# Two tiles' worth of lead for the projections of tile 5, and a second projection step per unit for tiles 4 to 7, in a graph-and-attention kernel

## The chip, the cores and the metric

The kernel runs on one core of one Trainium2 chip. The metric is the time of one execution on the device in microseconds. Instructions run on five engines that each work through their own queue in order: TensorE (PE, matmuls), VectorE (DVE), ScalarE (ACT), GpSimd (POOL) and SyncE (SP, which issues the DMAs). They wait for each other through semaphores.

## The reference, cut to what matters

Two layers run over 3327 nodes with 256 features. Each layer has a graph step over a dense 3327 x 3327 adjacency matrix and a feed-forward step: a mixture of experts in the first layer, and in the second a causal attention with four heads of width 64, each with four query "experts", followed by a small feed-forward part. The change touches only this last step:

```
sx = einsum('bsh,ndh->bnsd', x, hl_w) + hl_b
q = einsum('bnsd,neod->bneso', sx, wq)
k = einsum('bnsd,nod->bnso', sx, wk)
v = einsum('bnsd,nod->bnso', sx, wv)
scores = einsum('bnesd,bntd->bnest', q, k) * d ** 0.5 + causal
att = softmax(scores, axis=-1)
qkv = einsum('bnest,bntd->bnesd', att, v)
qkv = where(sx == 0, 0.0, qkv)
...
mixed = einsum('bnsed,bnse->bnsd', out.reshape(b, nh, s, ne, d), gs)
hn = layernorm(mixed + resid, ln_g, ln_b)
...
```

Here x is the normalised input, b is 1, n counts the heads, e the four query experts, s the query rows and t the key rows. All is computed in 32-bit floats.

## The kernel before, in words

The rows are cut into 26 tiles of 128 (NT). The second layer's last step is the function heads() at line 854, which takes from about 985 us to the end. Its engines are wrapped so that every engine keeps the order in which the program issues its instructions; the order written in the Python code is therefore the order in each queue.

*Units, chunks, rounds.* A unit is one tile t and one head h (line 1387). A unit's keys are cut into t // 4 + 1 chunks of up to 512 (span, line 1012), so tiles 0 to 3 have one chunk a unit, tiles 4 to 7 two, tiles 8 to 11 three. The main loop (line 1438) handles one chunk k per pass; this text calls a pass a round, and names chunks as tile.head.chunk, such as 4.1.0. A round does, in this order:

- drain_to(wanted(k)): VectorE copies scores from PSUM to SBUF with their maxima (drain, line 1034) until it is k + 3 + t // 4 chunks on; drains that find nothing filled call fill_next() first.
- attend(k) on TensorE: probabilities times values, into the PSUM tile po.
- turn(k + 1) on VectorE: the transpose of the next chunk's probabilities.
- values(k + 2): four DMAs on SP into vr (three buffers); weigh(k + 2): the exponentials on ScalarE, two ahead of the rest of the round and two behind it if the chunk is not a unit's first, else all four behind.
- back() of the unit that ended in the round before: TensorE turns its output (ptO), ScalarE copies it to qkv and glp.
- over(), if this chunk is the unit's last: po times a mask to ot, for tiles below 5 on VectorE, later by ScalarE and POOL.
- run(preps) and run(tails), if no unit ended in the round before or the tile is below 8: one step of each projection under way, and one step of each tail (norms and feed-forward of finished tiles).
- the rest of weigh(k + 2), and fill_next() (line 1407): TensorE multiplies queries and keys of the next chunk into four tiles pqk of PSUM (fill, line 1019).

*PSUM.* po takes four banks. The pool with the tag "b" has four buffers of a bank; pqk, all projections, transposes, ptO and the tails share it. One fill takes all four.

*Projections.* prepare() (line 907) is a generator with nine steps for a tile:

1. load x (SP)
2. statistics of its rows (three VectorE instructions)
3. power, subtract and multiply to xn (POOL)
4. transpose xn, evict to xt
5. psxt = hl_w times xt; sxt and the mask nz (four ScalarE instructions)
6. four DMAs sxd <- nz; pv, evict to v
7. pk, two evictions to kt; four DMAs vs <- v
8. pq, two evictions to qt (scaled by 8)
9. transpose of sxt, evict to sx

Only after step 9 does the tile's entry in ready hold qt. empty() (line 877) picks ScalarE or VectorE for an eviction by two running sums of estimated load. For tiles below AHEAD, qt is placed in a buffer of the pool "sc" (nine buffers, which otherwise hold the scores) and is called qts in the profile; for the others it has a tag of its own with two buffers.

*When a projection is begun.* begin(u) (line 1389) is called by fill_next() for a unit's first chunk. For head 0 of tile t it first calls run(preps) until the tile's qt is ready, and then begins other tiles: the next tile (t + 1) if that is AHEAD or more, and tile t + 2 if that is below AHEAD (tile 0 begins 1 and 2). With AHEAD = 5, tiles up to 4 are begun two tiles ahead, and tiles from 5 on are begun one tile ahead. As fills run four to five chunks ahead of attend in tiles 4 to 7, begin(5) falls into the round of chunk 4.2.0, begin(6) into that of 5.2.0, and so on; begin(4) falls into the round of 3.1.0.

Of the kernel before, what the change touches and what calls it, by code (L numbers as in the profile page):

```python
# [101 lines left out]
class Net:  # L102
# [751 lines left out]
    def heads(self, xs, vs, out):  # L854
# [3 lines left out]
        with ExitStack() as ctx:  # L858
# [48 lines left out]
            def prepare(t, res):  # L907
# [65 lines left out]
                yield  # L973
                if t < AHEAD:

# [20 lines left out]
            def run(gens):  # L996

                gens[:] = [g for g in gens if next(g, None) is None and g.gi_frame is not None]

            tails, preps, ready = [], [], {}  # L1000
            AHEAD = 5

            def later(n, gen):

# [14 lines left out]
            def fill(u, g):  # L1019

                t, h = u["t"], u["h"]
                lo, n = span(t, g)
                n *= P
                pq = u["pq"] = []
                for i in range(2):
                    pq += [ps.tile([P, BLK], F32, tag="b", name="pqk") for _ in range(2)]
                    for k in range(2):
                        r = ds(64 * k, 64)
                        nc.tensor.matmul(
                            pq[2 * i + k][:, :n], u["qt"][r, h, i, :], kt[r, h, ds(lo * P, n)],  # L1030
                            start=True, stop=True,
                        )
# [27 lines left out]
            def weigh(u, g, experts):  # L1060

                n = span(u["t"], g)[1] * P
                q = ready[u["t"]]
                if u["h"] == g == 0 and 0 in experts:
                    q["den"] = sm.tile([P, 16, 7], F32, tag="den", name="aden", bufs=2)
                for k in experts:
                    e = u["sc"][g][:, k, :n]
                    nc.scalar.activation(
                        e, e, AF.Exp, bias=u["nmax"][:, k : k + 1],
                        accum_out=q["den"][:, 4 * u["h"] + k, g : g + 1],  # L1070
                    )
                    load["act"] += 0.26 + 0.00088 * n

            def values(u, g):

                lo, n = (4 * i for i in span(u["t"], g))
                v = u["v", g] = vrp.tile([P, 16, 64], F32, tag="vr", name="vr")
                for q in range(4):
                    nc.sync.dma_start(out=v[ds(Q * q, Q), :n, :], in_=vs[u["h"], :, lo : lo + n, :])

            def turn(u, g):


                n = span(u["t"], g)[1] * P
                w = u["sc"][g][:, :, :n]
                nc.vector.transpose(w, w)
                load["dve"] += 0.1 + 0.00417 * n
# [7 lines left out]
            def attend(u, g):  # L1095


                t = u["t"]
                w, v = u["sc"][g], u["v", g]
                lo, n = (4 * i for i in span(t, g))  # L1100
                for b2 in range(0, n, 2):
                    for k in range(2):
                        for q in range(4):
                            r, b = ds(Q * q, Q), b2 + k

                            after = 4 * t + q - lo
                            if b > after and t:
                                continue
                            nc.tensor.matmul(
                                po[ds(64 * k, 64), q, :, :], v[r, b, :], w[r, :, ts(b, Q)],  # L1110
                                start=(g == b2 == 0), stop=(b + 2 > after if t else b2 == 2),
                            )

            def over(u):

                u["ot"] = tl.tile([P, 4, P], F32, tag="ot", name="ot", bufs=1)
                to = u["ot"].rearrange("p e (q i) -> p q e i", q=4)
                there = u["sxd"][:, u["h"] : u["h"] + 1, :]
                if u["t"] < 5 or u is units[-1]:

                    nc.vector.tensor_tensor(
                        to, po,
                        there.rearrange("p o (q i) -> p q o i", q=4).to_broadcast([P, 4, 4, Q]),
                        ALU.mult,
                    )
                    load["dve"] += 0.7
                else:
                    nc.scalar.copy(to, po)
                    nc.gpsimd.tensor_tensor(
                        u["ot"], u["ot"], there.to_broadcast([P, 4, P]), ALU.mult  # L1130
                    )
                    load["act"] += 0.6

            def back(u):


                h = u["h"]
                r = ready[u["t"]]
                if h == 0:
                    r["qkv"] = tl.tile([P, 4, 4, 64], F32, tag="qkv", name="qkv", bufs=2)  # L1140
                    r["glp"] = sm.tile([P, 4, 4, 4], F32, tag="glp", name="glp", bufs=3)
                pt = ps.tile([P, 4, 68], F32, tag="b", name="ptO")
                for e in range(4):
                    nc.tensor.matmul(
                        pt[:, e, :], u["ot"][:, e, :], igw[:, h, e, :], start=True, stop=True
                    )
                nc.scalar.copy(r["qkv"][:, h, :, :], pt[:, :, :64])
                nc.scalar.copy(r["glp"][:, h, :, :], pt[:, :, 64:])
                load["act"] += 0.55
                if u["t"] == NT - 1:  # L1150
                    if h % 2:
                        tails.append(last_tail(u["t"], h // 2, u["sx"], r))
                elif h == 3:
                    while len(tails) > 4:
                        run(tails)
                    tails.append(tail(u["t"], u["sx"], r["qkv"], r["glp"], r["den"]))
# [232 lines left out]
            def begin(u):  # L1389

                t = u["t"]
                if u["h"] == 0:
                    if t == 0:
                        for _ in prepare(0, ready.setdefault(0, {})):
                            pass
                    while preps and "qt" not in ready[t]:
                        run(preps)
                    begun = [t + 1] if AHEAD <= t + 1 < NT else []
                    if t + 2 < AHEAD:
                        begun = [t + 2] if t else [1, 2]  # L1400
                    for i, n in enumerate(begun):
                        preps.append(later(4 * i, prepare(n, ready.setdefault(n, {}))))
                u.update(ready[t])
# [3 lines left out]
            def fill_next():  # L1407
                nonlocal filled
                if filled < len(chunks):
                    u, g = chunks[filled]  # L1410
                    if g == 0:
                        begin(u)
                    fill(u, g)
                    filled += 1

            def drain_to(n):
                nonlocal drained
                while drained < min(n, len(chunks)):
                    if filled == drained:
                        fill_next()  # L1420
                    drain(*chunks[drained])
                    drained += 1

            def wanted(k):

                return k + 3 + chunks[min(k + 2, len(chunks) - 1)][0]["t"] // 4
# [11 lines left out]
            for k, (u, g) in enumerate(chunks):  # L1438
                ahead = chunks[k + 2] if k + 2 < len(chunks) else None
                drain_to(wanted(k))  # L1440
                attend(u, g)
                if k + 1 < len(chunks):
                    turn(*chunks[k + 1])
                if ahead:
                    values(*ahead)
                    if ahead[1]:
                        weigh(*ahead, range(2))
                if ended:
                    back(ended)
                last = u if g == u["t"] // 4 else None  # L1450
                if last:
                    over(u)
                if not ended or u["t"] < 8:
                    run(preps)
                    run(tails)
                ended = last
                if ahead:
                    weigh(*ahead, range(2 if ahead[1] else 0, 4))
                if filled == drained:
                    fill_next()  # L1460
            back(ended)
            while tails:
                run(tails)
# [2 lines left out]
class Experts:  # L1466
# [340 lines left out]
    def run(self, beside):  # L1807
        net, tc, S = self.net, self.tc, self.SLOTS
        nc = self.nc
        with ExitStack() as ctx:  # L1810
# [80 lines left out]

            AHEAD = 5
            for i in range(AHEAD):
                take(i)
# [4 lines left out]
            for i in range(S + 2):  # L1899
                if i + AHEAD == self.SURE:  # L1900
                    while rest:
# [115 lines left out]
```

## Time and profile before

| What | Value |
|---|---|
| Time, median of 3 runs (lowest to highest) | 2946.86 us (2946.50 to 2949.19) |
| Profiled execution | 2943.34 us |
| Its span, first to last instruction | 2941.60 us |
| Mean granted TensorE clock | 0.977 |
| Heads stage | about 985 us to the end |
| pq (step 8) of tiles 4, 5, 6, 7, 8 starts at | 1076.51, 1123.33, 1171.93, 1215.91, 1264.40 us |
| Evictions qts <- pq, qt <- pq | 10 (8 ScalarE, 2 VectorE), 42 (ScalarE) |

The page of a profile gives busy times of each engine, the chain of work that ended last, and the costliest groups of instructions. Besides it the trace can be asked for stretches of time (busy microseconds of each engine in each, with the granted clock), for the instructions of an engine in order of time with the wait ahead of each and what released it, and for sums of waits. In an order of time a line reads: start, duration (or that of the merged group), engine, line, operation, output <- inputs with shapes, count, and in brackets the idle time of the engine just before it with what ended it. Ends of matmuls are modelled. All work of the heads stage is recorded under line 61, that of the wrapper, so instructions are told apart by their tile names.

### The profile page before, as it was taken

How to read it: one execution, taken by the hardware profiler on the slowest of the kernel's cores; microseconds unless marked ns; L12 is line 12 of the kernel's file. 1: busy time of each engine (PE TensorE's matmuls, PEld its weight loads, DVE VectorE, ACT ScalarE, POOL GpSimd, SP SyncE). 2: the span in 40 equal slices, each digit the busy share in tenths (PEclk: the TensorE clock that was granted, in tenths of full speed). 3: DMA queues.
4: the chain of work that ended last, by engine and by line, in shares of the span. 5: the costliest groups of instructions: out<-in, count | busy, mean ns of one | idle time of the engine just before them, and what ended most of it. 6: DMA issues, size and time to landing. Idle time of an engine off the chain costs nothing. (4 is left out here: it accounts for less than half of the span.)

```text
span 2941.6 us, 125324 instructions
## 1 busy us (share of the span) xinstructions
PE 2652.3 (90%) x53422; PEld 1963.2 (67%) x53422; DVE 2398.5 (82%) x5619; ACT 1811.3 (62%) x5128; POOL 973.1 (33%) x1448
## 2 busy tenths in 40 slices
PE   7999988878989898999999999999989999999995
PEld 5878877757767676666666666666666666666664
DVE  5102643589999587889989999999999999999997
ACT  6420135555554477778777777777767677676674
POOL 5441634622141146544334323322122222122121
PEclk9999999999999799999999999999999999999998
DMA  9994568647775232333333433333433433433432
GB/s 372 357 322 148 176 209 279 209 171 264 268 250 177 73 92 75 115 97 116 115 103 109 123 112 110 113 114 110 123 113 109 117 115 115 117 115 108 116 110 78
DMA packets 258188, 449.70 MB, mean 153 GB/s; under 512 B 58816, under 2 KB 156608, under 8 KB 257504
## 3 DMA queue, kind: packets, MB, share of 16 engines
q1 hardware_dynamic: 245536, 417.50, 45.7%
q0 software_dynamic: 6576, 18.02, 1.6%
q8 instruction: 421, 6.90, 1.0%
q10 hardware_dynamic: 5520, 6.18, 0.7%
q14 instruction: 135, 1.11, 0.1%
HBM read 393.37 MB, written 25.88 MB: 143 GB/s over the span
## 5 line engine op out<-in xcount | busy, mean ns | idle before, releaser
L61 ACT ACTIVATE sc<-sc,anmax 128x512 f32<-128x512 f32 (+3 forms) x1568 | 1039.9, 668 | 109.0 <-DVE anmax L61 108.9
L61 PEld LDWEIGHTS po<-sc,vr 32*64 32x64 f32 x43728 | 661.1, 131 | 390.9 <-DVE sc L61 233.8
L61 PE MATMUL po<-sc,vr 32*64 32x128 f32 x43728 | 764.0, 275 | 113.6 <-DVE sc L61 74.8
L61 DVE STREAM_TRANSPOSE sc<-sc 128x2048 f32<-128x2048 f32 (+3 forms) x392 | 816.4, 2083 | 26.2 <-ACT sc L61 25.3
L61 PE MATMUL pqk<-kt,qt 64*128 64x512 f32 (+1 forms) x2944 | 738.4, 582 | 18.6 <-ACT qt L61 5.3
L61 DVE TENSOR_SCALAR_CACHE_REDUCE sc<-pqk 128x512 f32<-128x512 f32 (+2 forms) x1152 | 654.9, 623 | 51.2 <-PE pqk L61 49.7
L61 PEld LDWEIGHTS pqk<-kt,qt 64*128 64x128 f32 x2944 | 299.3, 185 | 230.3 <-issue 99.2
L61 PE MATMUL acc<-wh,p 128*128 128x259 f32 x1352 | 309.1, 386 | 35.6 <-DVE p L61 35.5
L61 PEld LDWEIGHTS acc<-wh,p 128*128 128x128 f32 x1352 | 253.3, 190 | 93.4 <-DVE p L61 53.4
L61 PE MATMUL acc<-y,pan 128*128 128x256 f32 x1352 | 304.3, 385 | 11.4 <-DMA pan<-in_adjt_dram 9.7
L61 ACT ACTIVATION_READ_ACCUMULATOR sc<-sc,anmax 128x1 f32 x1568 | 299.0, 191 | 0.0
L61 POOL TENSOR_TENSOR ot<-ot,sxd 128x512 f32<-128x512 f32 x83 | 105.7, 1273 | 582.2 <-ACT ot L61 568.8
L61 PEld LDWEIGHTS acc<-y,pan 128*128 128x128 f32 x1352 | 258.4, 193 | 52.4 <-issue 16.7
L61 DVE CUSTOM_DVE_ANT_0 sc<-pqk,mask 128x512 f32<-128x512 f32 (+3 forms) x416 | 242.3, 636 | 24.2 <-PE pqk L61 23.7
L61 ACT ACTIVATE u<-u,d 128x512 f32<-128x512 f32 (+1 forms) x182 | 125.2, 688 | 159.2 <-DVE u L61 159.0
L61 DVE SCALAR_TENSOR_TENSOR u<-bc,d 128x512 f32<-128x512 f32 (+1 forms) x182 | 136.1, 748 | 0.1
L61 DVE SCALAR_TENSOR_TENSOR p<-pan,u 128x512 f32<-128x512 f32 (+1 forms) x182 | 127.5, 701 | 10.3 <-PE acc L61 6.1
L61 ACT ACTIVATE junk<-ar 128x1664 bf16<-128x1664 f32 x52 | 82.7, 1591 | 65.2 <-DMA ar<-in_adj_dram 64.2
L61 ACT COPY qkv<-ptO 128x256 f32<-128x256 f32 x104 | 38.4, 369 | 136.2 <-PE ptO L61 136.0
L61 PE MATMUL ptO<-igw,ot 128*128 128x68 f32 x832 | 117.4, 284 | 4.5 <-issue 2.7
L61 PEld LDWEIGHTS ptO<-igw,ot 128*128 128x128 f32 x832 | 102.5, 193 | 23.3 <-issue 17.4
L61 DVE CUSTOM_DVE_ANT_0 sg<-sg,dst 128x1664 bf16<-128x1664 bf16 (+2 forms) x56 | 99.6, 1787 | 1.2 <-ACT dst L61 1.0
(340 smaller groups left out, 3024.8 us busy)
## 6 DMA issues: line engine op xcount, KB each, us to landing
vr<-vs SPq DMA_DIRECT2D x976, 128.0 KB
ar<-in_adj_dram SPq DMA_DIRECT2D x104, 832.0 KB
vr<-vs SPq DMA_DIRECT2D x544, 96.0 KB
pan<-in_adjt_dram SPq DMA_DIRECT2D x156, 256.0 KB
pan<-in_adjt_dram SPq DMA_DIRECT2D x26, 1024.0 KB
pan<-in_adjt_dram SPq DMA_DIRECT2D x20, 832.0 KB
w1e<-w SPq DMA_DIRECT2D x59, 256.0 KB
took<-places SPq DMA_DIRECT2D x59, 129.0 KB
```

The source lines that it names most:

```text
L61: made = make(*args, **kw)
```

## The change

AHEAD becomes 6. Tile 5 is thereby begun in begin(3), in the round of chunk 2.1.0, instead of in begin(4), and its qt is placed in the pool "sc". begin(4) begins nothing. At the end of each round that is a unit's last, in tiles 4 to 7, run(preps) is called once more, behind fill_next().

```
@@ -998,7 +998,7 @@
                 gens[:] = [g for g in gens if next(g, None) is None and g.gi_frame is not None]
 
             tails, preps, ready = [], [], {}
-            AHEAD = 5
+            AHEAD = 6
 
             def later(n, gen):
 
@@ -1458,6 +1458,9 @@
                     weigh(*ahead, range(2 if ahead[1] else 0, 4))
                 if filled == drained:
                     fill_next()
+                if last and 4 <= u["t"] < 8:
+
+                    run(preps)
             back(ended)
             while tails:
                 run(tails)
```

With these steps the order of the projections becomes, as it can be read off the loop (steps in brackets are those of the added call):

| Round | before | changed |
|---|---|---|
| 2.2.0 to 3.0.0 | tile 4: 6, 7, 8 | tile 4: 6, 7, 8; tile 5: 1, 2, 3 |
| 3.1.0 | tile 4: 9 | tile 4: 9; tile 5: 4 |
| 3.2.0, 3.3.0, 4.0.0 | tile 5: 1, 2, 3 | tile 5: 5, 6, 7 |
| 4.0.1 | tile 5: 4 | tile 5: 8 [9] |
| 4.1.0, 4.1.1 | tile 5: 5, 6 | none |
| 4.2.0 | tile 5: 7, then 8 and 9 in begin(5) | none |
| 4.2.1 | tile 6: 1 | tile 6: 1 [2] |
| 4.3.0, 4.3.1 | tile 6: 2, 3 | tile 6: 3, 4 [5] |
| 5.0.0, 5.0.1 | tile 6: 4, 5 | tile 6: 6, 7 [8] |
| 5.1.0, 5.1.1 | tile 6: 6, 7 | tile 6: 9, none |
| 5.2.0 | tile 6: 8, then 9 in begin(6) | none |

Tiles 7 and 8 follow the pattern of tile 6. Tile 9, before its first steps in the rounds of tile 7, gets two of the added calls (its steps 2 and 5); from tile 8 on the added call is not made.

More of the change, by code (lines that the diff above doesn't have):

```diff
@@ L1000, in heads @@
             tails, preps, ready = [], [], {}
-            AHEAD = 5
+            AHEAD = 6
             def later(n, gen):
@@ L1460, in heads @@
                     fill_next()
+                if last and 4 <= u["t"] < 8:
+                    run(preps)
             back(ended)
```

## The prediction

> **What bounds the kernel now.** I read the page's busy line first, then a table of stretches over the heads stage, then VectorE's, TensorE's and ScalarE's order of time around the tiles that the change names. All recorded work carries the helper's line 61, so I place it by tile names.
>
> Share of each engine over the span, from the page:
>
> ```profile
> PE 2652.3 (90%) x53422; PEld 1963.2 (67%) x53422; DVE 2398.5 (82%) x5619; ACT 1811.3 (62%) x5128; POOL 973.1 (33%) x1448
> ```
>
> No engine is full on average, so the stage decides. Stretches (start:end, length, then busy us of PE, weight loads, DVE, ACT, POOL with counts, granted clock, DMA share, GB/s):
>
> ```profile
> 1060.00:1100.00 40.00, 37.62 (x853) 27.79 (x852) 36.05 (x98) 29.38 (x98) 19.98 (x29) 1.00 0.28 78
> 1100.00:1140.00 40.00, 34.16 (x589) 24.83 (x588) 26.90 (x78) 30.59 (x115) 23.21 (x36) 0.91 0.29 81
> 1140.00:1180.00 40.00, 37.63 (x768) 26.55 (x768) 32.08 (x89) 30.84 (x107) 27.50 (x40) 0.96 0.28 80
> 1180.00:1220.00 40.00, 37.70 (x849) 26.36 (x848) 34.17 (x89) 30.92 (x102) 24.74 (x36) 1.00 0.38 107
> 2000.00:2400.00 400.00, 367.85 (x10904) 248.99 (x10890) 388.05 (x852) 283.36 (x861) 96.87 (x135) 1.00 0.39 114
> ```
>
> Late in the stage VectorE is the bound (388 of 400). In the stretch of tiles 4 to 8, PE (94%) and DVE (80 to 90%) are both near full and hand work to each other every round. One stretch falls out: 1100 to 1140, where DVE does 26.9 us, PE loses 3.5, and the clock was 0.91. VectorE's longest waits, in order of time (start, us, what, [wait <- releaser]):
>
> ```profile
> 1116.03 1.25 DVE L61 STREAM_TRANSPOSE sc<-sc 128x1024 f32<-128x1024 f32 x1 [2.96 <-ACT sc L61]
> 1121.57 0.38 DVE L61 TENSOR_REDUCE l1ns<-fx 128x4 f32<-128x256 f32 x1
> 1128.74 0.56 DVE L61 TENSOR_SCALAR_CACHE_REDUCE sc<-pqk 128x384 f32<-128x384 f32 x1 [6.79 <-PE pqk L61]
> ...
> 1174.72 0.56 DVE L61 TENSOR_SCALAR_CACHE_REDUCE sc<-pqk 128x384 f32<-128x384 f32 x1 [2.85 <-PE pqk L61]
> ...
> 1218.91 0.69 DVE L61 TENSOR_SCALAR_CACHE_REDUCE sc<-pqk 128x512 f32<-128x512 f32 x1 [1.33 <-PE pqk L61]
> ...
> 1267.19 0.56 DVE L61 TENSOR_SCALAR_CACHE_REDUCE sc<-pqk 128x384 f32<-128x384 f32 x1 [1.11 <-PE pqk L61]
> ```
>
> The last four are the first drain of tiles 5, 6, 7 and 8. TensorE before the one at 1128:
>
> ```profile
> 1117.51 1.18 PE L61 MATMUL pqk<-kt,qts 64*128 64x384 f32 x4 [1.91 <-ACT v L61]
> ...
> 1122.32 0.71 PE L61 MATMUL pk<-sxt,wk 64*128 64x128 f32 x8
> 1122.96 0.44 PE L61 MATMUL pt<-ident,fx 128*128 128x128 f32 x2
> 1123.33 1.31 PE L61 MATMUL pq<-sxt,wq 64*128 64x128 f32 x16
> 1124.57 0.44 PE L61 MATMUL pt<-ident,sxt 128*128 128x128 f32 x2
> 1127.79 1.97 PE L61 MATMUL pqk<-kt,qt 64*128 64x384 f32 x8 [2.78 <-ACT qt L61]
> ```
>
> The reader is to see steps 7 (pk), 8 (pq) and 9 (pt of sxt) of tile 5's preparation one behind the other, then PE waiting for ScalarE's eviction of qt, which stands in ScalarE's queue behind four exponentials.
>
> **What the Trainium skill says.** "TensorE: Matmul & The Clock Gate", Part 1, says that the array falls to half rate after an idle window of about 3.4 us and that the window is free-running. The trace agrees: in 8 us stretches the clock was 0.79 at 1116 to 1124, 0.81 at 1124 to 1132 and again 0.79 at 1164 to 1172, each behind a PE wait, and it was 1.00 after 1180. "PSUM — Partial Sum Buffer", Terms, gives a matmul output at most one bank of eight: po takes four, the pool "b" the other four, and one fill (4 pqk) takes all four, so any projection behind a fill waits for VectorE's first drain. "Perfetto Trace Analysis", Identifying the Most-Contended Engine, warns that PE's busy share is no measure of its headroom; so "PE near full" here is weaker evidence than the waits.
>
> **The change, part by part.** I walked the loop at line 1438 by hand; a round is one chunk. prepare() has nine steps, and each run(preps) makes one.
>
> *Tile 5 now.* Begun in begin(4), it makes steps 1 to 7 in seven rounds, and begin(5) makes 8 and 9 at once. *Changed:* begun in begin(3), it makes steps 1 to 8 in the eight rounds before 4.1.0, and 9 in the first added call. begin(5), three rounds on, finds it done. What goes:
> - The wait of 6.79. Without pk, pq and pt, PE's fill stands behind ptO and pt<-fx. DVE was free at 1121.95; PE's ptO began at 1120.51, and ptO 1.1, pt 0.4 and the first score pair 0.95 lead to about 1123.0. I leave 1.0 of the wait: 5.8 saved.
> - Of the 2.96 before the transpose at 1116: ScalarE had no gap from 1100.6 to 1118, and sxt 0.63, nz 0.84 and v 0.35 of tile 5 stood in that queue: 1.8 saved.
> - The slow clock behind it: attend's 84 matmuls took 2.84 instead of 1.64 at 1129.7, and DVE then waited 0.69 and 0.62. I take 0.7.
>
> Sum 8.3; bounds 4 (half the waits come back) to 11 (the waits, both slow windows).
>
> *What tile 5 costs earlier.* PE's six groups, 4.0 us from start to start (pt 0.3, psxt 1.05, pv 0.6, pk 0.65, pq 1.1, pt 0.3), and ScalarE's 3.8 us go to 1083 to 1106. ScalarE has 5.7 us of gaps there (1.10, 1.27, 1.26, 2.09 ahead of qkv) and takes it. PE shows gaps of 0.93, 0.51 and 0.50, so up to 2.1 is uncovered while DVE runs without a wait over 0.72. I take 1.0; bounds 0 to 2.1. The three VectorE instructions of step 2 (0.7 us) only change place. Step 3 goes to a POOL that idled 13 us before 1085. Its nine DMA issues pass earlier through SP, whose vr loads were waited for once, for 0.5 us, in 1120 to 1270: nothing. qt now lies in one of the nine "sc" buffers for ten rounds; drains run up to five chunks ahead, with tile 4's qt that makes seven: nothing. All evictions after tile 1 go to ScalarE (qt 42 of 42), and the order of load sums moves too little to alter that.
>
> *The added call for tiles 6 to 8.* Steps 2, 5 and 8 go behind the fill of a unit's last round; step 9 is made two rounds before the tile begins. Waits of 2.85, 1.33 and 1.11 (5.3 together) stand at these beginnings, but PE itself paused for only 0.31 us at each: it was busy with pq and pt (1.6 us), which remain to be done. Where PE sets the pace nothing is gained by moving them. Upper bound 5.3, and 1.7 more for half of the slow window at 1166. Against it: of the added calls eight hold matmuls (sx of 5; psxt and q of 6, 7, 8; psxt of 9). Each now stands between a fill and the next attend and needs a bank, or two for q, that DVE must first drain: 0.55 or 1.1 us, 6.0 in all (5 x 0.55 + 3 x 1.1) if DVE reaches the drain only when PE is done filling, nothing if DVE waits for the scores as at 1174. The eviction falls where ScalarE waits for ptO anyway (1.0 to 4.1 us before each qkv). I take 2.5 gained and 1.6 lost: 0.9; bounds -6 to +7.
>
> Sum: -8.3 + 1.0 - 0.9 = -8.2 us. The profiled execution took 2943.34 (span 2941.60 and 1.74 around it): 2935.1. The median shown is 2946.86, 3.5 above it; 8 off that gives 2939.
>
> **Rivals.** (1) *The wait is refilled, 0.33.* Around 1085 to 1106 PE and DVE are both near full, and tile 5's 4 us lengthen those rounds by 2.1; bank waits cost 3 to 4 beside a gain of 2 at tiles 6 to 8; half the slow windows stay (2 of the 8.3). -8.3 + 2 + 2.1 + 1.5 = -2.7: 2944. For it: the 94% of PE. Against: the clean gap at 1121 that belongs to ordering alone. Here too falls the case that the second edit does nothing, if its calls find an empty list; the walk shows that only one in four does.
> (2) *The added call blocks attend, 0.17, slower.* PE is in order, so psxt or q waiting for a bank keeps attend, back and the next fill behind it. Price: 6.0 for the drains; and if the pauses trip the slow clock once in each of the eight, eight windows of 3.4 us at half rate lose up to 1.7 us each, 13.6. -8.3 + 1.0 + 6.0 + 13.6 = +12; with half of the windows +5.5; middle +9: 2956. It decides from about 1.7 us a call: 8 x 1.7 less the 7.3 of tile 5 is 6.3, just over what counts as slower. For it: the pause of 1.91 for v at 1117 shows what one bank costs. Against: the eviction is off the fill's way here.
> (3) *All three beginnings pay too,* within the forecast: -8.3 + 1.0 - 5.3 = -12.6: 2934.
>
> **How the numbers follow.** This kernel's measurement tells 0.2%, 5.9 us, from no change. Forecast (with the third rival) 0.50: faster, 2939, its own range 2933 to 2941. First rival 0.33, within 0.2%. Second 0.17, slower; its smaller outcomes reach into the range. Range 2931 to 2952: below it lies only a gain beyond every bound but the last, above it most of the second rival.
>
> **What would show it.** Right: tile 5's first drain waits under 1.5 us instead of 6.79; qts has 12 evictions instead of 10 and qt 40 instead of 42; no slow clock between 1100 and 1135; pq of tile 5 about 1105; first drains of tiles 6 to 8 under 1 us. Wrong: new PE waits for banks directly behind a fill, with attend behind them; DVE busy below 34 of 40 in 1060 to 1100; the slow clock at new places in tiles 5 to 8.

## The result, and the profile after

The changed kernel takes 2961.21 us (median of 5, 2957.57 to 2966.76); the kernel before, timed beside it, 2946.86 (2944.14 to 2949.19). The ratio is 1.0043, 95% interval 1.0031 to 1.0056: slower by 0.43%, some 13 us. The profiled execution took 2957.57 us, span 2955.9, mean granted clock 0.972.

The busy line of the page after the change:

```profile
PE 2658.0 (90%) x53422; PEld 1969.3 (67%) x53422; DVE 2397.5 (81%) x5619; ACT 1808.9 (61%) x5128; POOL 973.1 (33%) x1448
```

Counts are those of before: nothing was added, work was moved. The loss is new idle time. The same stretches (busy us of PE, weight loads, DVE, ACT, POOL, then clock):

```profile
1060.00:1100.00 40.00, 36.94 (x794) 27.98 (x795) 34.23 (x90) 31.03 (x105) 19.55 (x29) 1.00 0.29 77
1100.00:1140.00 40.00, 34.10 (x644) 24.00 (x643) 29.74 (x88) 28.23 (x106) 23.70 (x37) 0.91 0.27 75
1140.00:1180.00 40.00, 37.60 (x771) 28.66 (x771) 28.82 (x84) 30.07 (x105) 24.65 (x36) 0.88 0.27 77
1180.00:1220.00 40.00, 34.83 (x740) 25.98 (x733) 29.72 (x79) 28.85 (x98) 19.80 (x31) 0.87 0.38 108
2000.00:2400.00 400.00, 368.45 (x10760) 249.35 (x10761) 387.02 (x847) 285.93 (x869) 98.09 (x136) 1.00 0.39 114
```

The late stage is as before. In 1100 to 1140 DVE does 2.8 us more, as it should without the wait of 6.79, but the clock is still 0.91, and from 1140 to 1220 DVE does 29 of 40 us where it did 32 and 34. Single lines of VectorE's order of time (what lies between them is left out), at the places that answer to those shown of before (the first drains of tiles 5, 6, 7 and 8 start at 1125.13, 1178.12, 1227.61 and 1276.37):

```profile
1125.13 0.54 DVE L61 TENSOR_SCALAR_CACHE_REDUCE sc<-pqk 128x384 f32<-128x384 f32 x1
1132.60 1.25 DVE L61 STREAM_TRANSPOSE sc<-sc 128x1024 f32<-128x1024 f32 x1 [5.48 <-ACT sc L61]
1178.12 0.56 DVE L61 TENSOR_SCALAR_CACHE_REDUCE sc<-pqk 128x384 f32<-128x384 f32 x1 [1.88 <-PE pqk L61]
1187.59 0.43 DVE L61 BATCH_NORM_STATS2 pst<-xres 128x6 f32<-128x256 f32 x1 [5.36 <-DMA xres<-xs]
1227.61 0.68 DVE L61 TENSOR_SCALAR_CACHE_REDUCE sc<-pqk 128x512 f32<-128x512 f32 x1
1235.74 0.43 DVE L61 BATCH_NORM_STATS2 pst<-xres 128x6 f32<-128x256 f32 x1 [3.62 <-DMA xres<-xs]
1276.37 0.55 DVE L61 TENSOR_SCALAR_CACHE_REDUCE sc<-pqk 128x384 f32<-128x384 f32 x1
1283.49 0.43 DVE L61 BATCH_NORM_STATS2 pst<-xres 128x6 f32<-128x256 f32 x1 [2.60 <-DMA xres<-xs]
```

Every wait that the change aimed at is gone or smaller. But each is followed by another one elsewhere: 5.48 for ScalarE where 6.79 went, then 5.36, 3.62 and 2.60 for a load of x, 11.6 together, where 2.85, 1.33 and 1.11 were. Counted from 0 in order, the n-th of these statistics instructions is tile n's, so the last three are tiles 7, 8 and 9. Before, none of them waited.

To see where time is lost and not only where an engine idles, I compared the start of each chunk's first drain in the two traces, and took the difference (after less before, us):

| Chunk | 3.1.0 | 4.3.0 | 5.0.0 | 5.0.1 | 6.0.0 | 6.0.1 | 7.0.0 | 7.0.1 | 8.0.0 | 8.0.1 | 8.1.2 | 9.2.0 |
|---|---|---|---|---|---|---|---|---|---|---|---|---|
| Difference | +2.0 | +5.3 | -3.6 | +1.2 | +3.4 | +9.1 | +8.7 | +12.6 | +9.2 | +12.2 | +15.9 | +15.1 |

The 2.0 at the left is there before the first changed round. Each first drain of a tile comes early against its neighbours, and the chunk after it gives the gain back and more. Below, "stage difference" is this measure from chunk 2.3.0 to chunk 9.2.0 alone (293.75 us before): +13.1 here, all of the loss. What follows chunk 9.2.0 differs between single profiles by several us, so a ratio of a few tenths of a percent and a stage difference of one profile need not agree exactly.

Besides the waits the clock is worse in this stage. Its stretch in one, before and then after:

```profile
1060.00:1300.00 240.00, 220.82 (x4957) 156.94 (x4959) 200.03 (x526) 183.35 (x618) 134.39 (x195) 0.98 0.33 93
1060.00:1300.00 240.00, 212.30 (x4567) 155.02 (x4568) 187.59 (x492) 173.16 (x588) 128.83 (x188) 0.92 0.31 88
```

By the clock's records TensorE ran at half rate for 10.2 us of this stretch before and for 37.5 after. In e1 to e16 below it was 6.8 to 37.5 us: 17.1 in e1, 30.7 in e3, 23.9 in e13, 6.8 in e15. No run takes a wait away and leaves the slow clock that goes with it, so how much of a loss is the wait and how much the clock stays open.

**The load.** POOL, SP, VectorE, TensorE and ScalarE around 1187:

```profile
1181.09 0.73 POOL L61 TENSOR_TENSOR fo<-fo,xend 128x256 f32<-128x256 f32 x1
```

```profile
1181.84 0.36 SPq L61 DMA_DIRECT2D out_dram<-fo  x1
1182.30 1.77 SPq L61 DMA_DIRECT2D vr<-vs  x4
1184.17 0.37 SPq L61 DMA_DIRECT2D xres<-xs  x1
```

```profile
1188.34 0.68 DVE L61 CUSTOM_DVE_ANT_0 sc<-pqk,mask 128x512 f32<-128x512 f32 x1
```

```profile
1189.17 1.95 PE L61 MATMUL ptO<-igw,ot 128*128 128x68 f32 x8 [4.37 <-POOL prs L61]
```

```profile
1191.16 0.37 ACT L61 COPY qkv<-ptO 128x256 f32<-128x256 f32 x1 [6.15 <-PE ptO L61]
```

The added call makes step 2 in the same round as step 1. SP issues the load at 1184.17, behind four vr and an output DMA, which waits until POOL has written fo (1181.09 and 0.73 more); x is there 3.4 us later (1187.59 less 1184.17). VectorE had been ready for it since 1182.23 (1187.59 less 5.36) and could do nothing else: the drain that empties the banks stands behind the statistics and starts at 1188.34. TensorE's ptO needs a bank, and the fill ahead of it had taken all four, so it had to wait for the first of these drains, which ends at 1189.02. The label says prs on POOL, but by the code ptO reads nothing of POOL's prs. ScalarE waits 6.15 for ptO. A single late load has stopped three engines.

**The mask.** ScalarE and POOL before VectorE's wait at 1132.60:

```profile
1129.73 0.42 ACT L61 ACTIVATE nzf<-fx 128x256 f32<-128x256 f32 x1 [5.12 <-POOL fo L61]
```

```profile
1128.98 0.73 POOL L61 TENSOR_TENSOR fo<-fo,nzf 128x256 f32<-128x256 f32 x1
```

and ScalarE's same instruction before:

```profile
1124.43 0.42 ACT L61 ACTIVATE nzf<-fx 128x256 f32<-128x256 f32 x1 [0.44 <-POOL fo L61]
```

nzf (line 1242) has one buffer. The tail of one tile writes its mask into it while POOL has yet to read the mask of the tile before. ScalarE waits 5.12 for that, with the exponentials behind it that the transpose at 1132.60 needs. Before, ScalarE waited only 0.44 for the same mask, inside the 6.79 that VectorE spent on tile 5's projection (1121.95 to 1128.74). With the change ScalarE is ready for it 0.6 us later (1124.61 against 1123.99), but POOL, at work without a pause since 1113.73, reads the old mask 5.3 us later (1128.98 against 1123.66). Why POOL came so much later was not looked into.

### The profile page after: what moved, and what is told of

It reads as the page before. It is cut to its first block, busy times and chain, and to the rows that moved or that the text cites. A ratio compares the mean times of both kernels' runs of the same rounds, so it can differ in the third digit from the quotient of the medians.

```text
span 2955.9 us, 125326 instructions
## 1 busy us (share of the span) xinstructions
PE 2658.0 (90%) x53422; PEld 1969.3 (67%) x53422; DVE 2397.5 (81%) x5619; ACT 1808.9 (61%) x5128; POOL 973.1 (33%) x1448
## 3 DMA queue, kind: packets, MB, share of 16 engines
q14 instruction: 135, 1.11, 0.1%
## 5 line engine op out<-in xcount | busy, mean ns | idle before, releaser
L61 PE MATMUL pqk<-kt,qt 64*128 64x512 f32 (+1 forms) x2880 | 722.0, 587 | 18.6 <-DVE sc L61 8.2
```

Source lines behind the costliest of these rows:

```text
L61: made = make(*args, **kw)
```

## The experiments

All ratios are to the kernel before, run on the same chip; e1 to e16 ran on three chips, on which it took 2941 to 2949 us, so where an expectation is in us it is read as a ratio to 2946.86. Stage differences are worked out from the drains' starts as above.

| Run | Edit, against after | Ratio [95%] | Stage difference |
|---|---|---|---|
| after | | 1.0043 [1.0031, 1.0056] | +13.1 |
| e1 | without the added call | 1.0008 [0.9999, 1.0017] | +1.9 |
| e2 | AHEAD 5 | 1.0034 [1.0023, 1.0045] | +8.8 |
| e3 | x loaded one round earlier | 1.0015 [1.0008, 1.0022] | +5.4 |
| e4 | no call in head 2 | 1.0057 [1.0043, 1.0071] | +19.6 |
| e5 | call in head 1 of tiles 5 to 7 only | 0.9996 [0.9987, 1.0004] | +1.1 |
| e6 | e1 with the mask later | 0.9995 [0.9988, 1.0002] | -3.8 |
| e7 | before with the mask later | 0.9998 [0.9990, 1.0006] | +0.8 |
| e8, e16 | e5 with the mask later | 0.9991 [0.9983, 0.9999], 0.9992 [0.9984, 1.0001] | -6.6, -4.6 |
| e9 | without tile 9's two calls | 1.0036 [1.0021, 1.0051] | +5.8 |
| e10 | e3, no call in head 3 | 1.0041 [1.0030, 1.0053] | +14.1 |
| e11 | AHEAD 5, fewer calls | 0.9985 [0.9973, 0.9997] | -2.2 |
| e12 | e11 with the mask later | 1.0002 [0.9989, 1.0014] | -6.2 |
| e13 | x loaded a whole tile earlier | 1.0002 [0.9994, 1.0010] | +1.8 |
| e14 | e13 without tile 9's calls | 0.9992 [0.9984, 1.0000] | -2.6 |
| e15 | e14 with the mask later | 0.9982 [0.9974, 0.9990] | -8.5 |

Where an expectation gives the three load waits to tiles 6, 7 and 8, they are those of tiles 7, 8 and 9, as counted above; the places are the same.

### The two edits apart: e1, e2

e1 leaves out the added call, e2 leaves AHEAD at 5.

```
-                if last and 4 <= u["t"] < 8:
-
-                    run(preps)
```

```
-            AHEAD = 6
+            AHEAD = 5
```

> AHEAD = 6 alone, without the added call. Three theories stand. Load: in the added call, step 2 of tiles 7, 8 and 9 stands directly behind its own load of x, and VectorE waits for the DMA (5.36, 3.62 and 2.60 us in the changed kernel), with the slow clock behind it. Bank: the matmul steps of the added call wait for PSUM banks behind a fill and hold attend up. Mask: tile 5's lead removes the wait of 6.79 us, but ScalarE then waits 5.1 us for the single buffer nzf, which POOL still reads. Load and bank both expect the 14 us to be gone here: 2945 to 2951 us. Mask expects no gain over before either, 2946 to 2950, with a VectorE wait of 4 to 6 us before the transpose in the round of 4.2.1; without mask the gain of tile 5 would show: 2939 to 2942. If the lead of tile 5 is itself the damage: 2957 or more.

> The added call alone, AHEAD = 5. Tile 5, begun in begin(4), then gets two added steps and is done before begin(5), so the wait of 6.79 us at its first drain should go here too. Load expects the three VectorE waits for xres (2.5 to 5.5 us each) at tiles 6, 7 and 8 unchanged, and a time of 2954 to 2962. Bank expects the same time but without it resting on these waits. If the lead of tile 5 were the damage: 2940 to 2948.

e1 came out as the kernel before, e2 slower by 0.34%: the added call is the greater part of the loss. Neither result is one effect alone. In e1 tile 5 gains 5.6 us up to chunk 5.0.0 and gives back 7.1 by 6.0.0, at the mask and in the slow clock behind it:

```profile
1127.71 1.25 DVE L61 STREAM_TRANSPOSE sc<-sc 128x1024 f32<-128x1024 f32 x1 [5.46 <-ACT sc L61]
```

e2 has the load's waits of 5.13, 3.08 and 2.54 us as after has. It also shows that tile 5 did not need the longer lead: with the added call alone its first drain waits 2.07, no long wait for the mask follows, and the 5.1 us gained from 2.3.0 to 6.0.0 are lost only behind 6.0.0.

### The load: e3, e13

e3 takes the load out of the generator and issues it in begin(), one round before the statistics; e13 issues it when the projection of the tile before is begun, 44 us or more ahead of the statistics.

```
+            def fetch(t):
                 x = tl.tile([P, D], F32, tag="xres", name="xres", bufs=2)
                 nc.sync.dma_start(out=x, in_=xs[ts(t, P), :])
+                return x
...
+                        x = fetch(n) if n > 5 else None
+                        preps.append(later(4 * i, prepare(n, ready.setdefault(n, {}), x)))
```

```
+                        x = fetched.pop(n, None)
+                        if 5 <= n < 9:
+                            fetched[n + 1] = fetch(n + 1)
```

> The changed kernel with one thing moved: for tiles 6 and up the load of x is issued in begin(), one round ahead; step 1 of the projection then does nothing, and all other steps stay where they are. Load expects no VectorE wait for xres over 0.5 us and 2945 to 2952 us (11.6 us of waits and some slow clock gone). Bank expects 2957 or more, since every matmul stands where it stood.

> The changed kernel, and x of tiles 6 to 9 loaded a whole tile earlier, in the begin() before the one that begins its projection. The load one round earlier had left waits of 1.2 to 3.9 us, since SP's queue stood behind an output DMA. No other step moves. Load expects no VectorE wait for xres over 0.3 us at tiles 6 to 8, 7 to 11 us less than the changed kernel (1.0043): a ratio of 1.0005 to 1.002. Bank, or a loss from the order of the matmul steps at tiles 6 and 7, expects 1.003 or more.

e3 took back some two thirds of the loss, e13 practically all of it: 1.0043 became 1.0002, and the intervals lie apart. That is a little more than was expected of e13, and e3's waits of 1.22 and 1.13 are over the 0.5 that was allowed. Only the place of the load differs; every matmul step of the added call stays where the change put it. VectorE's order of time in e3, then in e13, for tiles 7 and 8:

```profile
1179.76 0.43 DVE L61 BATCH_NORM_STATS2 pst<-xres 128x6 f32<-128x256 f32 x1 [1.22 <-DMA xres<-xs]
1224.96 0.43 DVE L61 BATCH_NORM_STATS2 pst<-xres 128x6 f32<-128x256 f32 x1 [1.13 <-DMA xres<-xs]
```

```profile
1180.93 0.42 DVE L61 BATCH_NORM_STATS2 pst<-xres 128x6 f32<-128x256 f32 x1
1224.83 0.41 DVE L61 BATCH_NORM_STATS2 pst<-xres 128x6 f32<-128x256 f32 x1
```

SP's order of time in e3 says why one round is not enough: the load still stands behind the output DMA.

```profile
1176.98 0.36 SPq L61 DMA_DIRECT2D out_dram<-fo  x1
1177.44 0.38 SPq L61 DMA_DIRECT2D xres<-xs  x1
1177.91 2.02 SPq L61 DMA_DIRECT2D vr<-vs  x4
```

Here x is ready 2.3 us after its issue (1179.76 less 1177.44), against 3.4 behind four vr. The Trainium skill, "DMA: Bandwidth & Descriptors", Anatomy of one DMA, gives a fixed 2.0 us and bytes over 436 GB/s, fitted for GpSimd's path: an estimate of 2.3 for 128 KB, as e3 measures on SP's. Its Rules for kernel authors say to issue early and wait late; in e13 a whole tile was enough, where in e3 one round was not.

What e13 still loses: 7.1 us between 5.0.0 and 6.0.0 (the mask), and 4.2 between 8.0.0 and 9.2.0. It gains 5.6 up to 5.0.0 and 0.7 and 3.2 over tiles 6 and 7.

### Fewer calls: e4, e10

The other way to part step 1 from step 2 is to leave out the call that makes step 2. In e10 head 3's call goes, with e3's load.

```
-                if last and 4 <= u["t"] < 8:
+                if last and 4 <= u["t"] < 8 and u["h"] != 2:
```

```
-                if last and 4 <= u["t"] < 8:
+                if last and 4 <= u["t"] < 8 and u["h"] != 3:
```

> The changed kernel without the added call in head 2 (tiles 4 to 7), where it makes step 2. The added calls of heads 3 and 0 remain and make steps 4 and 7 (transpose of xn, keys), both with matmuls directly behind a fill. Load expects 2945 to 2952 and no wait for xres over 0.5 us. Bank expects 2956 or more.

> The kernel with the earlier load, and in addition without the added calls of head 3, where step 5 (psxt) needs the xt that step 4 has only just sent to ScalarE. What remains are steps 2 (its x loaded before) and 7 (pk, independent of 6). Pair expects the 4.1 us that the earlier load alone lost at tile 8 to fall by at least 2, and a ratio of 0.9995 to 1.0008 to before (1.0015 with these calls). Bank expects a matmul behind the fill to go on costing: 1.001 or more.

What load and pair expected failed in both runs; in time both came out as the theory of the banks had it (1.0057 and 1.0041). In e4 the trace shows another cause. The steps behind the missing one come in other pairs: step 4 now stands in the same round as step 3, and TensorE waits for POOL as VectorE had waited for SP. TensorE's order of time in e4:

```profile
1191.09 0.44 PE L61 MATMUL pt<-ident,xn 128*128 128x128 f32 x2 [1.58 <-POOL xn L61]
1237.69 0.44 PE L61 MATMUL pt<-ident,xn 128*128 128x128 f32 x2 [3.32 <-POOL xn L61]
1294.91 0.69 PE L61 MATMUL pt<-ident,xn 128*128 128x128 f32 x2 [4.04 <-POOL xn L61]
```

So it is not step 2 alone that is dear: step 4 is, too, where its input is made in its own round. It is not so of every such pair, as step 5 stands in one round with step 4 in e13 as well, and tiles 6 and 7 lose nothing there. In e10 one load still waited 3.89, and TensorE waited for banks elsewhere; which of its pairs costs how much I did not settle.

### Tile 9's calls: e9, e14

```
-                if last and 4 <= u["t"] < 8:
+                if last and 4 <= u["t"] < 8 and (u["t"], u["h"]) not in ((7, 2), (7, 3)):
```

> The changed kernel without the two added calls that serve tile 9 (7.2.1 and 7.3.1); those for tiles 5 to 8 stay. In the changed kernel 5.9 us were lost between the first drain of tile 8 and tile 9. Pair expects that this loss is theirs (2.6 for x, a slow clock behind it, and psxt that needs xt in the same round): under 2 us left there, and a ratio of 1.001 to 1.003 to before, 0.0015 to 0.003 under the changed kernel. If the loss comes from the steps of tile 8 being done early, it stays at 4 us or more.

> The same without the two added calls for tile 9. If the losses are these three and no more (x at tiles 6 to 8, tile 9's steps pulled forward, and the wait for nzf at tile 5), the rest of the added call costs nothing and the time is that of AHEAD = 6 alone or a little less: a ratio of 0.999 to 1.0008. If the matmul steps behind a fill cost something of their own: 1.0015 or more.

The stage between 8.0.0 and 9.2.0 goes from +5.9 to -0.2 in e9, and from +4.2 to -0.1 in e14. The ratios move by less than their intervals (e14 against e13 0.10%, e9 against after 0.07%), and e9's is above what was expected of it. What these calls do can be seen with the load out of the way. TensorE, then VectorE, in e13:

```profile
1284.37 1.14 PE L61 MATMUL pqk<-kt,qt 64*128 64x384 f32 x2 [0.94 <-ACT xt L61]
1285.44 2.07 PE L61 MATMUL psxt<-xt,hlt 128*128 128x128 f32 x8
1287.44 2.07 PE L61 MATMUL po<-sc,vr 32*64 32x128 f32 x96
1289.44 1.11 PE L61 MATMUL ptO<-igw,ot 128*128 128x68 f32 x8
1290.48 1.56 PE L61 MATMUL pqk<-kt,qt 64*128 64x384 f32 x8
```

```profile
1291.42 0.56 DVE L61 CUSTOM_DVE_ANT_0 sc<-pqk,mask 128x384 f32<-128x384 f32 x1 [3.62 <-PE pqk L61]
```

and VectorE at the same drain in e14:

```profile
1288.18 0.56 DVE L61 CUSTOM_DVE_ANT_0 sc<-pqk,mask 128x384 f32<-128x384 f32 x1
```

In e13 the fill waits for a bank that ScalarE's xt gives back, then psxt stands between fill and attend, and the next fill comes 3.3 us later (1290.48 against 1287.23 in e14): VectorE runs dry. This is the second rival's mechanism, at one place. The clock has a part in it: from 1284 to 1292 it was 0.79 in e13 and 1.00 in e14.

### The second call only where it pays: e5, e11

e5 makes it in head 1 of tiles 5 to 7 alone (step 8 of the next tile); e11 has AHEAD 5 as well, and the call in (4, 0).

```
-                if last and 4 <= u["t"] < 8:
+                if last and 5 <= u["t"] < 8 and u["h"] == 1:
```

```
+                if last and 4 <= u["t"] < 8 and (u["h"] == 1 or (u["t"], u["h"]) == (4, 0)):
```

> AHEAD = 6, and the added call only in head 1 of tiles 5 to 7. There it makes step 8 (queries, two banks, behind a fill), whose input sxt has been ready for rounds; step 9 follows a round on, ahead of begin(). Theory of the pair, as the four runs so far have left it: an added call costs where its step needs the result of the step made in the same round (load and statistics; POOL's xn and its transpose; xt and psxt), and not otherwise. It expects no new wait over 1 us in tiles 5 to 8, first drains of tiles 6, 7 and 8 that wait under 1.5 us (3.03, 1.22, 1.11 with AHEAD = 6 alone), and 0 to 5 us less than AHEAD = 6 alone: a ratio of 0.999 to 1.001 to before. Bank expects each of the three calls to cost 1 to 2 us: 1.002 or more.

> A version from the findings: AHEAD = 5 as before, the added call in heads 0 and 1 of tile 4 (tile 5 makes steps 5 and 8 there and is done before begin(5)) and in head 1 of tiles 5 to 7. In the run with the call alone tile 5 gained 5.0 us up to the first drain of tile 6, without the long wait for nzf. Expected if pair holds: tile 5 gains 3 to 5, tiles 6 to 8 0 to 2, a ratio of 0.9978 to 0.9995 to before. If bank decides, 1.000 or more.

e5 is as fast as before, no faster; its first drain of tile 6 still waits 2.25, and VectorE's wait behind the mask is there (5.50). e11 is faster by 0.15%, with an interval from 0.03 to 0.27%. Neither has a load in one round with its statistics, and in e11 no long wait for the mask comes up.

### The mask: e6, e7, e8, e16, e12, e15

The first mask of a tail is made one step later, when POOL has had a round more to read the one before:

```
-                nonzero(nz[:, 0, :], fx)
                 yield
+                nonzero(nz[:, 0, :], fx)
                 nonzero(nz[:, 1, :], fxt.rearrange("p c q -> p (c q)"))
```

> AHEAD = 6 alone, and in the tails the mask nz of fx is made one step later, so that ScalarE does not stand in front of the exponentials of 4.2.1 waiting for the buffer nzf. Mask expects the VectorE wait of 5.46 us before the transpose in that round to fall under 2 and the gain of tile 5 to show: a ratio of 0.997 to 0.999 to before. If the wait comes from something else in ScalarE's queue, it stays at 4 to 6 us and the ratio at 1.000 to 1.002.

> The kernel before with the same later mask, AHEAD = 5: what this edit does by itself. Mask expects little, 0.999 to 1.001, since the wait for nzf lies there inside the wait of 6.79 us for the scores of tile 5. If the later mask helps everywhere: 0.998 or less.

> The two together: AHEAD = 6, the added call only in head 1 of tiles 5 to 7, and the later mask. Pair and mask together expect the sum of both gains, 5 to 9 us below before: a ratio of 0.997 to 0.9985. If one of them is wrong, 1.000 or more.

> The version with AHEAD = 6, the added call in head 1 of tiles 5 to 7 and the later mask once more (0.9991 with an interval of 0.9983 to 0.9999 the first time): 0.998 to 1.000.

> The same with the mask nz of fx made one step later in the tails. Expected: 0.9975 to 0.999 to before, at best a little under the run with AHEAD = 6, head 1 and the later mask (0.9991). If the later mask helps only where tile 5 has its longer lead, no difference to the same kernel without it.

> The same with the later mask, which takes the third loss away: 0.997 to 0.999 if all three are what ate the gain; 1.000 or more if not.

In e6 VectorE's wait of 5.46 is gone from that place; the longest left there is this:

```profile
1134.07 0.42 DVE L61 TENSOR_REDUCE l2ns<-fo 128x4 f32<-128x256 f32 x1 [1.72 <-POOL fo L61]
```

The stage difference goes from +1.9 (e1) to -3.8. In the kernel before, the same edit brings nothing (e7), since VectorE waits there for the projection anyway. So in the stage the mask, with the slow clock behind it (17.1 us at half rate in e1, 6.8 in e6), is what swallowed tile 5's gain, and it can be seen only once that wait is gone. As a ratio e6 is not apart from before, where 0.997 to 0.999 was expected. e12 missed: its stage is better than e11's by 4.0, its ratio is not better. It lost time behind chunk 9.2.0 in its profile, for a reason that I do not know. e8 and its repeat e16 agree, at 0.9991 and 0.9992: less than the 0.997 to 0.9985 that was expected of e8, though its stage difference is as expected.

e15 has all three cures. It has the lowest ratio of all runs, 0.9982 [0.9974, 0.9990]. Its interval lies wholly below that of e13, but overlaps those of e14 and e11, so as a ratio the third cure is not shown by itself. Its stretches:

```profile
1100.00:1140.00 40.00, 36.40 (x697) 25.78 (x701) 32.45 (x95) 32.59 (x125) 26.39 (x40) 1.00 0.31 87
1140.00:1180.00 40.00, 37.83 (x855) 27.51 (x840) 31.70 (x91) 32.03 (x112) 27.57 (x41) 0.96 0.28 80
1180.00:1220.00 40.00, 39.44 (x876) 28.01 (x876) 34.97 (x88) 32.56 (x107) 23.54 (x35) 1.00 0.38 110
```

The clock in 1100 to 1140 is 1.00 where before and after had 0.91, and PE does 36.4 us where they had 34.2 and 34.1.

## Why the prediction was wrong

The forecast was 2939 us, in a range of 2931 to 2952; 2961.21 was measured.

- *Tile 5's wait.* Right in its place and size: the first drain waits 0.00 instead of 6.79, pq of tile 5 starts at 1108.14 (about 1105 was named), qts has 12 evictions, and the tile's first drain comes 5.6 us earlier in 5.0.0 both in e1 and after (differences taken from chunk 2.3.0). Predicted were 8.3 less 1.0, which is 7.3. Of the parts, the wait of 6.79 gave all; the 2.96 ahead of the transpose gave 1.1, not 1.8 (1.82 is left); and tile 5's earlier steps cost 3.3 up to chunk 4.3.0 in e1 and after, where 1.0 was taken and 2.1 was the bound.
- *What is late next.* The prediction left this out for tile 5, and there it was the mask: 7.1 us given back in e1 by chunk 6.0.0. Of that the slow clock is part; the 0.7 for its going was not had, as 1100 to 1140 still shows 0.91.
- *The step that failed* is the costing of the added call. It counted only the calls that hold matmuls, "eight hold matmuls", each at a bank's price, and let steps without matmuls go free: "The three VectorE instructions of step 2 (0.7 us) only change place" and of the DMAs "nothing" had been reasoned for tile 5, where step 2 keeps a round of its own. Behind the added call it does not: the table of the change shows "tile 6: 1 [2]", load and statistics in one round. The term of 1.6 lost thus lacked the wait on VectorE, measured at 11.6 us in three places, and the slow clock behind it. With the load moved and nothing else, the stage improves by 11.3 (from +13.1 to +1.8) and the ratio by 0.41%, about 12 us of 2946.86; the time at half rate falls from 37.5 to 23.9 us with it.
- *Tiles 6 to 8.* First drains of under 1 us were named; two wait nothing, tile 6's 1.88. Their gain is real where the load is out of the way: e14 gains 3.9 over tiles 6 and 7 (0.7 and 3.2) where 0.9 was predicted in all. The matmul steps behind a fill cost these tiles nothing net.
- *The rivals.* The sign was the second rival's, its mechanism only in part. Banks held behind a fill did cost at tile 9's psxt (4.3 us in e13 against e14, with a slow clock in it), in one place and not in eight, so the 6.0 of its price is not what was lost. Two of its signs came: TensorE waits for a bank behind a fill (4.37 at 1189.17), but because the load held up VectorE's drain, and the slow clock stands at new places. So its other price, eight slow windows of 3.4 us, came in number: 27.3 us more at half rate is eight times 3.4. But they stand behind waits for the mask and a load, up to four in a row, and not one behind each call. The first rival, in which the wait is refilled, describes e1 well (1.0008, no change), by the mask and in part by tile 5's steps in earlier rounds (3.3, where it had 2.1). Its sum takes 2 us for slow windows out of a gain that holds 0.7 for them.
- *The sum.* e15 takes the three losses away and shows -8.5 us in the stage against the predicted -8.2; over the whole kernel its ratio stands for -5.3 us (0.18% of 2945.77). That the sums agree is luck in good part: e15 has three edits that the prediction had not, tiles 6 to 8 gave more, and tile 5 less, than was said.

## What to carry to other kernels

Before a second step of a pipeline is put into a round, ask which step makes its input, and whether that step is now in the same round: here an engine that works in order then waited 2.6 to 5.4 us for a load and 1.6 to 4.0 us for POOL, with everything queued behind it. A wait that is removed can uncover or lengthen another beside it (0.44 us for the mask became 5.12), so look for single-buffered tiles whose readers and writers the wait had kept apart. A load that has a buffer can be issued a whole tile early, for which e13 shows no price; one round was too little here, where its queue also carries output.

## What the runs showed of the hardware

**One pause of 4 us, some 12 us at half speed.** Clock (after the last busy time) by stretches of 2 us after the change, from within TensorE's wait of 4.06, which ends at 1134.07, on (the five stretches left out read 0.50):

```profile
1130.00:1132.00 2.00, 0.00 (x1) 0.00 (x0) 0.00 (x0) 1.97 (x9) 0.50 (x1) 1.00 0.02 4
1132.00:1134.00 2.00, 0.00 (x0) 0.00 (x0) 1.41 (x2) 2.00 (x9) 0.00 (x0) 0.63 0.00 0
1134.00:1136.00 2.00, 1.93 (x4) 0.99 (x4) 1.93 (x8) 1.90 (x9) 0.44 (x1) 0.50 0.00 0
...
1146.00:1148.00 2.00, 2.00 (x41) 1.58 (x30) 1.70 (x2) 1.41 (x6) 1.42 (x3) 0.96 0.19 47
```

TensorE shows no gap from 1134.07 on, and still ran at 0.50 until about 1146. After the wait of 4.37 that ends at 1189.17 it is the same (the four stretches left out read 0.50):

```profile
1186.00:1188.00 2.00, 0.00 (x0) 0.00 (x0) 0.41 (x1) 0.00 (x0) 0.00 (x0) 0.78 0.46 134
...
1196.00:1198.00 2.00, 2.00 (x56) 1.53 (x42) 1.56 (x1) 1.54 (x5) 0.00 (x0) 0.66 0.04 8
```

It ran at 0.50 to about 1197.4, eight matmuls of ptO in 1.95 us instead of 1.11. The Trainium skill, "TensorE: Matmul & The Clock Gate", Part 1, gives full speed back after about 3.4 us of sustained work; here it took 12 and 8.2 us from TensorE's restart, and the measurement decides. Matmul ends are modelled, so how busy the array was in between is not shown.

Worked out from the means, the first stay at half speed is 13.6 us: (1 - 0.63) x 4 in the stretch from 1132, six stretches of 2 us, and 0.2 at the end. The second is 10.2 (0.78 from 1186, four stretches at 0.50, 0.66 from 1196). Before, the stay at 1128 to 1134 (0.74, 0.50, 0.90) was 3.4. These are close to four, three and one times 3.4. So the prediction's window had the right length, but one pause can be followed by several; its 0.7 us for the slow clock and its second rival counted one. The pause can also be shorter than the window: ahead of the three slow stays that the prediction read as agreeing with an idle window of 3.4 us, TensorE had waited 1.91, 2.78 and 1.02.

**The same load took 2.3 or 3.4 us** from issue to use, according to whether four small DMAs were issued ahead of it on the same queue or behind it. One case each, so that is what was seen and not a rule.
